# A routed expert layer on one core: the first tiles' totals and table ahead of the second part's gates, one-hot rows in halves, ties by a running count, rows three tiles ahead

## The chip, the cores and the metric

The kernel runs on one core of a Trainium2 chip. The metric is device time in microseconds; the figure before the change is the median of three runs. One further execution was taken with the hardware profiler, and all durations below come from it. Its engines are PE (TensorE, matmuls), DVE (VectorE), ACT (ScalarE), POOL (GpSimd) and SP (SyncE, which here issues DMAs).

## The reference

There are 64 x 64 = 4096 tokens of 256 values. Each token goes to the two of eight experts with the largest gates, and the result is added to the token.

```python
var = jnp.mean(x * x, axis=-1, keepdims=True)
xn = rms_w * (x * jax.lax.rsqrt(var + EPS))
gate = xn @ wg_W + wg_b + (genre_embed @ gg_W + gg_b)
gate_w = jax.nn.softmax(gate, axis=-1)
topk_w, topk_i = jax.lax.top_k(gate_w, TOP_K)
cw = jnp.sum(jax.nn.one_hot(topk_i, E, dtype=x.dtype) * topk_w[..., None], axis=-2)
h1 = jax.nn.relu(jnp.einsum('bsh,ehm->bsem', x, W1) + b1)
h2 = jax.nn.relu(jnp.einsum('bsem,emn->bsen', h1, W2) + b2)
out_e = jnp.einsum('bsen,enh->bseh', h2, W3) + b3
x + jnp.einsum('bseh,bse->bsh', out_e, cw)
```

With equal gates the expert with the smaller number is taken. H is 256, M is 512, everything is f32.

## The kernel before

**Layout.** Each of 128 partitions holds 32 tokens, so there are 32 token tiles (NI), in eight loads of four (`load j`, `xin[j]`). The first eight token tiles (two loads, NA = 8, GA = 2) are part A, the other 24 part B. Part A is routed first, so that the expert work can start on it while part B is still being routed.

**Routing.** For a load j and a half c of the 256 columns, `turn` (L183) transposes four 128x128 blocks on PE (L187) into one of the PSUM banks `TB` and copies them to a buffer `hid[:, n]` (L189 on DVE, L191 on ACT). `gates` (L193) multiplies such buffers by the gate weights; the q-th buffer writes PSUM partitions 32q to 32q+31 (L196), and the two column halves are added up there. `upright` (L204) copies the gates to `gTs` on ACT (L207) and transposes them back on PE (L210). `squares` (L176) makes a token tile's sum of squares, on ACT (L179) or on DVE (L181). `busy(n)` (L213) puts n transposes on PE whose result nobody reads (L216).

**The class Part** holds the routing of one part: `choose` (L251) scales the gates and finds the largest two in two rounds. A round takes the maximum, compares (L274), multiplies by `rank` (8 for expert 0 down to 1, L276), takes the maximum (L278) and compares again (L280), so that one expert is left of equal ones. `count` (L286) makes running counts of tokens per expert along a partition (L290), `totals` (L299) adds them over the partitions on PE (L302, L303), `pick` (L305) reads each token's place.

**The first part** (L343) does this for part A. Its table is made by one-hot rows: `ohA` (L405, 128 x 16 f16 values in each partition) says which row a token goes to, `mvA` (L406) holds its number, and 16 small matmuls (L423) sum them up in PSUM. From that DVE makes `idxA` (L425, L426), the token numbers of eight tiles of 128 tokens, one per expert. Between these steps stand the transposes, copies and gates of loads 2 to 5.

**The second part** (L428) does the transposes and gates of loads 6 and 7, the transpose of the bias vectors (`vecs`, L443, copied to `vT` by L444), and most of the sums of squares. L777 does the last four.

**The rest of part B's routing** is the generator `rest` (L456). `head_step` (L713) takes pieces of it while it works on the first seven tiles; `routing(ns)` takes pieces until their stated costs reach ns. It ends in `idxR`, the token numbers of all further tiles, and in the weights store (L328).

**The tiles.** 67 tiles of 128 tokens run in this profile: eight of part A, and 59 of the rest. For a tile, POOL gathers 128 rows of x (`gather` L585, DMA at L576) into one of three buffers `xg`, PE transposes them (L597), DVE copies them to `xTb` (L599), and PE does layer 1 (L659), layer 2 (L672) and layer 3 (L684), with ACT's relu between (L662, L675). DVE scales the result (L685), POOL adds it to the output rows by DMA (L686). From tile 8 on, DVE first copies the expert's weights (L625, L633, L644), and POOL gathers the tile's gate weights (`gather_cw` L589) that DVE reads at L647. `step(s)` (L737) issues layer 1 of tile s, the transposes of s + 1, layer 2 of s - 1, layer 3 of s - 2; its gather is that of tile s + 2. `head_step` gathers s + 3.

**Order.** In the blocks under `manual_schedule` the order of each engine's work is that of the program. That is so for the first part, the gathers of tiles 0 to 2, the second part, `busy(18)` (L788), the head steps and step 7, and again for the last steps. The steps between are ordered by a scheduler. The last tiles stand in a switch over the number of tiles.

Of the kernel before, what the change touches and what calls it, by code (L numbers as in the profile page):

```python
# [9 lines left out]
F32 = mybir.dt.float32  # L10
# [3 lines left out]
ALU = mybir.AluOpType  # L14
# [7 lines left out]
def kernel(  # L22
# [92 lines left out]
    nc.gpsimd.memset(ones, 1.0)  # L115
    rank = const.tile([P, E], F32, name="rank")
    nc.gpsimd.iota(rank, [[-1, E]], base=E, channel_multiplier=0, allow_small_or_imprecise_dtypes=True)
    tri = const.tile([P, P], F32, name="tri")
# [7 lines left out]
    nc.gpsimd.memset(segA, 1.0)  # L126
    nc.gpsimd.memset(segA[:, :, 0:1], 0.0)
    iotx = const.tile([P, P, GC], F16, name="iotx")
    nc.gpsimd.iota(iotx, [[1, P], [0, GC]], base=0, channel_multiplier=0, allow_small_or_imprecise_dtypes=True)
# [53 lines left out]
    def turn(j, c, n, eng):  # L183

        tp, xTc = TB[n], hid[:, n].rearrange("p c t -> p (c t)")
        for k in range(TPB):
            nc.tensor.transpose(tp[:, ts(k, P)], xin[j][:, k, ts(c, P)], ident)  # L187
        if eng == "V":
            V.tensor_copy(xTc, tp)  # L189
        else:  # L190
            nc.scalar.copy(xTc, tp)  # L191

    def gates(c, bufs, bank=PB[3]):  # L193

        for q, n in enumerate(bufs):
            nc.tensor.matmul(  # L196
                bank[32 * q : 32 * q + 32, :],
                lhsT=wg_sb[:, c, :],
                rhs=hid[:, n].rearrange("p c t -> p (c t)"),
                start=(c == 0),  # L200
                stop=(c == HC - 1),
            )

    def upright(nq, bank=PB[3], dst=PB[4]):  # L204

        R = 32 * nq
        nc.scalar.copy(gTs[0:R, :], bank[0:R, :])  # L207
        gtp = dst[:, 0 : TPB * R].rearrange("p (k r) -> p k r", k=TPB)
        for k in range(TPB):
            nc.tensor.transpose(gtp[:, k], gTs[0:R, ts(k, P)], ident[0:R, 0:R])  # L210
        return gtp.rearrange("p k (q e) -> p q k e", q=nq)[:, :, :, 0:E]
# [6 lines left out]
    class Part:  # L218


        def __init__(self, z, i0, i1):
            self.i0, self.i1, self.n, self.z = i0, i1, i1 - i0, z
            n = self.n
            self.t = {a: t2(f"{a}{z}", n) for a in ("var", "root", "y", "t", "rstd", "m1", "m2", "top", "den", "d2")}
# [26 lines left out]
        def choose(self, raw):  # L251

            m1, m2, top = (self.t[a] for a in ("m1", "m2", "top"))
            gate, left, rstd = self.gate, self.pr[:, 0], self.t["rstd"]
            if raw is None:
# [12 lines left out]
            for k, (g, m) in enumerate(((gate, m1), (left, m2))):  # L268
# [6 lines left out]
                yield  # L275
                V.tensor_tensor(sc, sc, self.over_i(rank), ALU.mult)  # L276
                yield
                V.tensor_reduce(top, sc, AX.X, ALU.max)  # L278
                yield
                V.tensor_tensor(sc, sc, self.over_e(top), ALU.is_equal)  # L280
                yield
# [61 lines left out]
    def first_part():  # L343
# [27 lines left out]
        V.tensor_copy(ggate, gps)  # L371
        gates(0, (0, 2))
        gates(1, (1, 3))
        pA.root()
# [12 lines left out]


        for q in range(4):
            turn(GA + q, 0, q, "A")  # L390
        gates(0, range(4))
        squares(NA, "A")
        squares(NA + 1, "A")
        for _ in pA.choose(raw):
            pass
        pA.count()
        for q in range(2):
            turn(GA + q, 1, q, "A")
        pA.totals()
        slot = pA.gate  # L400
        V.scalar_tensor_tensor(
            slot, pA.inc.rearrange("p e i -> p i e"), -1.0, pA.over_i(pA.off[:, 0, :]), ALU.add, ALU.add
        )
        pA.pick(lo16A.rearrange("p (k i) -> p k i", k=TOPK), slot)
        V.tensor_tensor(ohA, iotx, lo16A.unsqueeze(1).to_broadcast([P, P, GC]), ALU.is_equal)  # L405
        V.tensor_tensor(  # L406
# [4 lines left out]
        )  # L411
        V.tensor_copy(totA, pA.off[:, 1, :])
        for q in range(2, 4):
            turn(GA + q, 1, q, "A")
        squares(NA + 2, "A")
        gates(1, range(4))
        raw = upright(4)
        nc.scalar.copy(graw[:, NA : NA + 4 * TPB, :].rearrange("p (q k) e -> p q k e", q=4), raw)
        squares(NA + 3, "A")
        squares(NA + 4, "A")  # L420
        tabA = PB[7][:, 0:E]
        for g in range(GC):
            nc.tensor.matmul(tabA, lhsT=ohA[:, :, g], rhs=mvA[:, g, :], start=(g == 0), stop=(g == GC - 1))  # L423

        V.tensor_scalar(sa[:, 0:E], tabA, 0.0, float(NT), ALU.is_equal, ALU.mult)  # L425
        V.scalar_tensor_tensor(idxA, tabA, float(OFFA), sa[:, 0:E], ALU.add, ALU.add)  # L426

    def second_part():  # L428

        j0 = GA + 4  # L430
        for i in range(NA + 8, NI - 4):
# [9 lines left out]
        nc.scalar.copy(graw[:, j0 * TPB : NI, :].rearrange("p (q k) e -> p q k e", q=2), raw)  # L441
        vps = PB[6][:, 384 : 384 + 2 * E * MC]
        nc.tensor.transpose(vps, vecs, ident[: 2 * E * MC, : 2 * E * MC])  # L443
        V.tensor_copy(vT.rearrange("p l e c -> p (l e c)"), vps)  # L444
        for i in range(NA + 5, NA + 8):
            squares(i, "A")

# [8 lines left out]
    def rest():  # L456
# [85 lines left out]
        V.tensor_tensor(idxR, sa, sb, ALU.add)  # L542
        gather(E)
        pB.exps()
        yield 1000
# [191 lines left out]
    def step(s, last):  # L737

        if s + 2 < last:
            gather(s + 2)  # L740
        if s < last:
# [30 lines left out]
    with tc.manual_schedule():  # L772
        first_part()
        for b in range(3):
            gather(b)
        second_part()
        for i in range(NI - 4, NI):  # L777
# [9 lines left out]

        busy(18)  # L788
        routing(100)
# [66 lines left out]
```

## Time and profile before

| what | us |
|---|---|
| median of 3 runs | 543.44 (543.28 to 543.70) |
| the profiled execution's own time | 539.8 |
| its span, first to last instruction | 538.0 |
| busy PE / weight loads / DVE / ACT / POOL | 522.7 / 499.3 / 286.8 / 215.6 / 285.2 |
| mean granted PE clock | 0.994 |
| first tile's layer 1 starts | 31.92 |
| PE's last matmul starts (L684) | 525.95 |

Times in the profile count from the span's start. A line of the timeline has the start, the duration, the engine, the line of the program, the operation, out<-in by the program's names, shapes and the number of instructions merged; the bracket has the idle time of the engine before it and what ended it. An f32 matmul is two instructions, a transpose one. Matmuls overlap, so the distance from start to start says more than a duration. The timed runs lie 3.6 us above the profiled execution.

### The profile page before, as it was taken

To read this page: it belongs to the slowest core of one execution; us is meant where nothing else is said; L and a number is where in the kernel's file an instruction comes from. 1 tells how busy PE (TensorE), PEld (TensorE's weight loads), DVE (VectorE), ACT (ScalarE), POOL (GpSimd) and SP (SyncE) were. 2 spreads that over 40 slices of the span, in tenths; PEclk is the share of its full clock that TensorE was granted. 3 is DMA by queue.
4 is the path that set the end of the run, shared out by engine and by line. 5 is a ranking of instruction groups with operands and counts; after the bars stand their busy time and mean duration, and the time that the engine had idled before them with its cause. 6 is when DMAs were issued, how large, how long until landed. Compare 5 with 4: busy or idle time off the path is not lost. (4 is left out here: it accounts for less than half of the span.)

```text
span 538.0 us, 11373 instructions
## 1 busy us (share of the span) xinstructions
PE 522.7 (97%) x4136; PEld 499.3 (93%) x4136; DVE 286.8 (53%) x651; ACT 215.6 (40%) x588; POOL 285.2 (53%) x237
## 2 busy tenths in 40 slices
PE   8989999999999999999999999999999999999992
PEld 6579999999999999999999999999999999999992
DVE  4686964455455555554554545555545555454540
ACT  3754333343344434344444344344334434433430
POOL 4233668775565555556555556555556554236542
PEclk9999999999999999999999999999999999999997
DMA  8999976122222212222212221222222212222221
GB/s 272 383 393 371 367 197 177 29 41 41 41 34 31 38 33 37 39 41 31 37 28 40 41 41 26 40 32 39 31 42 34 38 28 35 30 33 39 32 22 22
DMA packets 28650, 44.45 MB, mean 83 GB/s; under 512 B 6161, under 2 KB 18530, under 8 KB 28324
## 3 DMA queue, kind: packets, MB, share of 16 engines
q0 software_dynamic: 15136, 17.32, 20.8%
q1 hardware_dynamic: 12736, 26.25, 13.8%
q8 instruction: 34, 0.56, 0.4%
q14 instruction: 36, 0.29, 0.2%
q10 hardware_dynamic: 708, 0.03, 0.1%
HBM read 35.33 MB, written 13.24 MB: 90 GB/s over the span
## 5 line engine op out<-in xcount | busy, mean ns | idle before, releaser
L672 PE MATMUL pb<-hid,big 128*128 128x128 f32 x1888 | 220.6, 275 | 0.0
L672 PEld LDWEIGHTS pb<-hid,big 128*128 128x128 f32 x1888 | 215.6, 192 | 0.3 <-ACT hid L662 0.2
L686 POOL DMA_INDIRECT out_dram<-y,idxR x59 | 106.2, 1801 | 157.4 <-DVE y L685 153.3
L675 ACT ACTIVATE hid<-pb,bb 128x128 f32<-128x128 f32 x236 | 86.8, 368 | 140.4 <-PE pb L672 96.2
L633 DVE COPY big<-w2a 128x2048 f32 x59 | 72.7, 1232 | 122.5 <-issue 75.7
L662 ACT ACTIVATE hid<-pb,bb 128x128 f32<-128x128 f32 x236 | 86.4, 368 | 121.2 <-PE pb L659 102.3
L659 PEld LDWEIGHTS pb<-xTb,big 128*128 128x128 f32 x944 | 114.7, 192 | 3.1
L659 PE MATMUL pb<-xTb,big 128*128 128x128 f32 x944 | 114.9, 275 | 0.0
L684 PE MATMUL pb<-big,hid 128*128 128x256 f32 x472 | 111.7, 379 | 0.0
L684 PEld LDWEIGHTS pb<-big,hid 128*128 128x128 f32 x472 | 85.2, 190 | 9.1
L576 POOL DMA_INDIRECT cg<-cwdR,idxR x59 | 72.5, 1229 | 21.3 <-issue 16.9
L576 POOL DMA_INDIRECT xg<-in_x_dram,idxR x59 | 60.9, 1033 | 19.7 <-issue 14.6
L599 DVE COPY xTb<-pb 128x256 f32<-128x256 f32 x67 | 28.4, 424 | 41.1 <-PE pb L597 35.7
L685 DVE SCALAR_TENSOR_TENSOR y<-pb,cw,bc 128x256 f32<-128x256 f32 x59 | 28.5, 484 | 36.0 <-PE pb L684 36.0
L625 DVE COPY big<-w1a 128x1024 f32 x59 | 41.0, 695 | 5.3 <-DVE xTb L599 0.9
L644 DVE COPY big<-w3a 128x1024 f32 x59 | 40.3, 683 | 0.0
L672 PE MATMUL pb<-hid,w2a 128*128 128x128 f32 x256 | 29.9, 275 | 0.0
L672 PEld LDWEIGHTS pb<-hid,w2a 128*128 128x128 f32 x256 | 29.2, 192 | 0.0
L597 PE MATMUL pb<-ident,xg 128*128 128x128 f32 x134 | 25.7, 273 | 0.5 <-DMA xg<-in_x_dram,idxR 0.5
L686 POOL DMA_INDIRECT out_dram<-y,idxA x8 | 14.0, 1755 | 15.5 <-DVE sli L505 7.0
L649 DVE TENSOR_SCALAR bc<-b_sb,cw 128x256 f32 x59 | 20.8, 353 | 0.4
L675 ACT ACTIVATE hid<-pb,vT 128x128 f32<-128x128 f32 x32 | 11.7, 368 | 18.7 <-PE pb L672 18.1
(184 smaller groups left out, 279.4 us busy)
## 6 DMA issues: line engine op xcount, KB each, us to landing
w2a<-in_L_cond_W_dram SPq DMA_DIRECT2D x8, 1024.0 KB
big<-in_x_dram SPq DMA_DIRECT2D x8, 512.0 KB
w1a<-in_L_cond_W_dram SPq DMA_DIRECT2D x8, 512.0 KB
w3a<-in_L_cond_W_dram SPq DMA_DIRECT2D x8, 512.0 KB
out_dram<-in_x_dram SPq DMA_DIRECT2D x4, 768.0 KB
out_dram<-in_x_dram SPq DMA_DIRECT2D x1, 1024.0 KB
b_sb<-in_L_cond_b_dram SPq DMA_DIRECT2D x1, 1024.0 KB
xg<-in_x_dram,idxR POOLq DMA_INDIRECT x59
```

The lines of the kernel that those rows point to most:

```text
L576: nc.gpsimd.indirect_dma_start(out=dst, out_offset=None, in_=src, in_offset=bass.IndirectOffsetOnAxis(ap=index(b), axis=0), bounds_check=N ...
L599: V.tensor_copy(xTb, tp)
L625: V.tensor_copy(w1, w1a[:, e].rearrange("p e c m -> p (e c) m"))
L633: V.tensor_copy(w2, w2a[:, ex[b]].rearrange("p e c m -> p (e c) m"))
L644: V.tensor_copy(w3, w3a[:, e].rearrange("p e c m -> p (e c) m"))
L659: nc.tensor.matmul(ph, lhsT=w1[:, c, ts(m, P)], rhs=xTb[:, c, :], start=(c == 0), stop=(c == HC - 1))
L662: nc.scalar.activation(h1[:, m, :], ph, AF.Relu, bias=bb[:, 0, m : m + 1])
L672: nc.tensor.matmul(ph, lhsT=w2[:, m, ts(n, P)], rhs=h1[:, m, :], start=(m == 0), stop=(m == MC - 1))
L675: nc.scalar.activation(h2[:, n, :], ph, AF.Relu, bias=bb[:, 1, n : n + 1])
L684: nc.tensor.matmul(po, lhsT=h2[:, n, :], rhs=w3[:, n, :], start=(n == 0), stop=(n == MC - 1))
L685: V.scalar_tensor_tensor(y, po, cw, bc, ALU.mult, ALU.add)
L686: add = nc.gpsimd.indirect_dma_start(out=orows, out_offset=bass.IndirectOffsetOnAxis(ap=index(b), axis=0), in_=y, in_offset=None, bounds_c ...
```

## The change

- Ties: `rank` goes. After the comparison a running count along the experts (a scan over `segT`, which is 0 at expert 0 and 1 elsewhere) numbers the equal ones, and one fused operation keeps the one with number 1.
- The gates of part A go quadrant by quadrant, both column halves of one load and then of the next.
- In the first part two ACT squares stand ahead of the transposes of loads 2 to 5. The totals stand ahead of all transposes of the second column half, `mvA` behind the totals, `ohA` is made in two halves of eight groups with eight table matmuls behind each, and the table stands ahead of the second half's gates. `totA` is copied last.
- In the second part ACT's copy to `gTs` and PE's first eight transposes stand ahead of `upright`; the transpose of `vecs` follows it, and its copy stands within the squares. Two more squares are on ACT and two fewer on DVE. `busy(2)` goes; the later `busy(18)` is `busy(16)`.
- `rest` gathers tile 9 right behind tile 8, and `step` gathers tile s + 3.

```diff
-    rank = const.tile([P, E], F32, name="rank")
-    nc.gpsimd.iota(rank, [[-1, E]], base=E, channel_multiplier=0, allow_small_or_imprecise_dtypes=True)
+    segT = const.tile([P, NB, E], F32, name="segT")
+    nc.gpsimd.memset(segT, 1.0)
+    nc.gpsimd.memset(segT[:, :, 0:1], 0.0)
...
-    def gates(c, bufs, bank=PB[3]):
-        for q, n in enumerate(bufs):
+    def gates(c, bufs, bank=PB[3], q0=0):
+        for q, n in enumerate(bufs, q0):
...
-                V.tensor_tensor(sc, sc, self.over_i(rank), ALU.mult)
+                V.tensor_tensor_scan(
+                    nth.rearrange("p i e -> p (i e)"),
+                    segT[:, 0 : self.n].rearrange("p i e -> p (i e)"),
+                    sc.rearrange("p i e -> p (i e)"),
+                    0.0,
+                    ALU.mult,
+                    ALU.add,
+                )
                 yield
-                V.tensor_reduce(top, sc, AX.X, ALU.max)
-                yield
-                V.tensor_tensor(sc, sc, self.over_e(top), ALU.is_equal)
+                V.scalar_tensor_tensor(sc, nth, 1.0, sc, ALU.is_equal, ALU.mult)
                 yield
...
-        gates(0, (0, 2))
-        gates(1, (1, 3))
+        for q in range(GA):
+            for c in range(HC):
+                gates(c, (2 * q + c,), q0=q)
...
+        some(2)
         for q in range(4):
             turn(GA + q, 0, q, "A")
         gates(0, range(4))
-        squares(NA, "A")
-        squares(NA + 1, "A")
+        some(2)
         for _ in pA.choose(raw):
             pass
         pA.count()
-        for q in range(2):
-            turn(GA + q, 1, q, "A")
         pA.totals()
...
-        V.tensor_tensor(ohA, iotx, lo16A.unsqueeze(1).to_broadcast([P, P, GC]), ALU.is_equal)
...
-        V.tensor_copy(totA, pA.off[:, 1, :])
-        for q in range(2, 4):
+        for q in range(4):
             turn(GA + q, 1, q, "A")
-        squares(NA + 2, "A")
...
+        tabA = PB[7][:, 0:E]
+        GH = GC // 2
+        for g0 in range(0, GC, GH):
+            hs = slice(g0, g0 + GH)
+            V.tensor_tensor(
+                ohA[:, :, hs], iotx[:, :, hs], lo16A[:, hs].unsqueeze(1).to_broadcast([P, P, GH]), ALU.is_equal
+            )
+            for g in range(g0, g0 + GH):
+                nc.tensor.matmul(tabA, lhsT=ohA[:, :, g], rhs=mvA[:, g, :], start=(g == 0), stop=(g == GC - 1))
+        some(3)
         gates(1, range(4))
-        raw = upright(4)
-        nc.scalar.copy(graw[:, NA : NA + 4 * TPB, :].rearrange("p (q k) e -> p q k e", q=4), raw)
-        squares(NA + 3, "A")
-        squares(NA + 4, "A")
-        tabA = PB[7][:, 0:E]
-        for g in range(GC):
-            nc.tensor.matmul(tabA, lhsT=ohA[:, :, g], rhs=mvA[:, g, :], start=(g == 0), stop=(g == GC - 1))
...
+        nc.scalar.copy(gTs, PB[3])
+        for q in range(2):
+            turn_pe(j0 + q, 0, q)
+        raw = upright(4, copied=True)
+        vps = PB[6][:, 384 : 384 + 2 * E * MC]
+        nc.tensor.transpose(vps, vecs, ident[: 2 * E * MC, : 2 * E * MC])
+        for i in range(NA + 10, NI - 4):
+            if i == NI - 8:
+                V.tensor_copy(vT.rearrange("p l e c -> p (l e c)"), vps)
             squares(i, "V")
-        for c in range(HC):
-            for q in range(2):
-                turn(j0 + q, c, 2 * c + q, "A")
+        for q in range(2):
+            turn_copy(q, "A")
+        nc.scalar.copy(graw[:, NA : NA + 4 * TPB, :].rearrange("p (q k) e -> p q k e", q=4), raw)
+        for q in range(2):
+            turn(j0 + q, 1, 2 + q, "A")
+        some(3)
         for c in range(HC):
             gates(c, (2 * c, 2 * c + 1), PB[7])
         busy(4)
         raw = upright(2, PB[7], PB[6])
-        busy(2)
         nc.scalar.copy(graw[:, j0 * TPB : NI, :].rearrange("p (q k) e -> p q k e", q=2), raw)
-        vps = PB[6][:, 384 : 384 + 2 * E * MC]
-        nc.tensor.transpose(vps, vecs, ident[: 2 * E * MC, : 2 * E * MC])
-        V.tensor_copy(vT.rearrange("p l e c -> p (l e c)"), vps)
-        for i in range(NA + 5, NA + 8):
-            squares(i, "A")
...
         gather(E)
+        gather(E + 1)
...
-        if s + 2 < last:
-            gather(s + 2)
+        if s + 3 < max(last, SURE + 1):
+            gather(s + 3)
...
-        busy(18)
+        busy(16)
```

`turn_pe` and `turn_copy` are the two halves of `turn`, and `some(n)` puts the next n squares on ACT.

More of the change, by code (lines that the diff above doesn't have):

```diff
@@ L183, in turn, with turn_pe, turn_copy @@
     def turn(j, c, n, eng):
+        turn_pe(j, c, n)
+        turn_copy(n, eng)
+    def turn_pe(j, c, n):
+        for k in range(TPB):
+            nc.tensor.transpose(TB[n][:, ts(k, P)], xin[j][:, k, ts(c, P)], ident)
+    def turn_copy(n, eng):
         tp, xTc = TB[n], hid[:, n].rearrange("p c t -> p (c t)")
-        for k in range(TPB):
-            nc.tensor.transpose(tp[:, ts(k, P)], xin[j][:, k, ts(c, P)], ident)
         if eng == "V":
@@ L202, in gates, with upright @@
             )
-    def upright(nq, bank=PB[3], dst=PB[4]):
+    def upright(nq, bank=PB[3], dst=PB[4], copied=False):
         R = 32 * nq
-        nc.scalar.copy(gTs[0:R, :], bank[0:R, :])
+        if not copied:
+            nc.scalar.copy(gTs[0:R, :], bank[0:R, :])
         gtp = dst[:, 0 : TPB * R].rearrange("p (k r) -> p k r", k=TPB)
@@ L223, in __init__ @@
             n = self.n
-            self.t = {a: t2(f"{a}{z}", n) for a in ("var", "root", "y", "t", "rstd", "m1", "m2", "top", "den", "d2")}
+            self.t = {a: t2(f"{a}{z}", n) for a in ("var", "root", "y", "t", "rstd", "m1", "m2", "den", "d2")}
             self.gate, self.w = t3(f"gate{z}", n), t3(f"w{z}", n)
@@ L251, in choose @@
         def choose(self, raw):
-            m1, m2, top = (self.t[a] for a in ("m1", "m2", "top"))
+            m1, m2 = self.t["m1"], self.t["m2"]
             gate, left, rstd = self.gate, self.pr[:, 0], self.t["rstd"]
+            nth = self.pr[:, 1]
             if raw is None:
@@ L386, in first_part, with some @@
             load_weights(e)
+        sA = iter(range(NA, NA + 10))
+        def some(n):
+            for _ in range(n):
+                squares(next(sA), "A")
+        some(2)
         for q in range(4):
@@ L396, in first_part @@
         pA.count()
-        for q in range(2):
-            turn(GA + q, 1, q, "A")
         pA.totals()
[L400 to L405, printed above, removed]
         V.tensor_tensor(
@@ L411, in first_part @@
         )
-        V.tensor_copy(totA, pA.off[:, 1, :])
-        for q in range(2, 4):
+        for q in range(4):
             turn(GA + q, 1, q, "A")
-        squares(NA + 2, "A")
-        gates(1, range(4))
-        raw = upright(4)
-        nc.scalar.copy(graw[:, NA : NA + 4 * TPB, :].rearrange("p (q k) e -> p q k e", q=4), raw)
-        squares(NA + 3, "A")
-        squares(NA + 4, "A")
-        tabA = PB[7][:, 0:E]
-        for g in range(GC):
-            nc.tensor.matmul(tabA, lhsT=ohA[:, :, g], rhs=mvA[:, g, :], start=(g == 0), stop=(g == GC - 1))
+        slot = pA.gate
@@ new lines, in first_part @@
+        V.scalar_tensor_tensor(
+            slot, pA.inc.rearrange("p e i -> p i e"), -1.0, pA.over_i(pA.off[:, 0, :]), ALU.add, ALU.add
+        )
+        pA.pick(lo16A.rearrange("p (k i) -> p k i", k=TOPK), slot)
+        tabA = PB[7][:, 0:E]
[4 more added lines that the diff above has]
+                ohA[:, :, hs], iotx[:, :, hs], lo16A[:, hs].unsqueeze(1).to_broadcast([P, P, GH]), ALU.is_equal
+            )
+            for g in range(g0, g0 + GH):
+                nc.tensor.matmul(tabA, lhsT=ohA[:, :, g], rhs=mvA[:, g, :], start=(g == 0), stop=(g == GC - 1))
@@ L425, in first_part, with second_part @@
+        some(3)
+        gates(1, range(4))
         V.tensor_scalar(sa[:, 0:E], tabA, 0.0, float(NT), ALU.is_equal, ALU.mult)
         V.scalar_tensor_tensor(idxA, tabA, float(OFFA), sa[:, 0:E], ALU.add, ALU.add)
-    def second_part():
+        V.tensor_copy(totA, pA.off[:, 1, :])
+        return some
+    def second_part(some):
         j0 = GA + 4
-        for i in range(NA + 8, NI - 4):
-            squares(i, "V")
-        for c in range(HC):
-            for q in range(2):
-                turn(j0 + q, c, 2 * c + q, "A")
+        nc.scalar.copy(gTs, PB[3])
[7 more added lines that the diff above has]
+                V.tensor_copy(vT.rearrange("p l e c -> p (l e c)"), vps)
+            squares(i, "V")
+        for q in range(2):
[4 more added lines that the diff above has]
+        some(3)
@@ L772 @@
     with tc.manual_schedule():
-        first_part()
+        some = first_part()
         for b in range(3):
             gather(b)
-        second_part()
+        second_part(some)
         for i in range(NI - 4, NI):
```

## The prediction

> **What bounds the kernel now.** I read busy time by stretch first, then TensorE's (PE's) queue over the first 32 us, then the queues of VectorE (DVE) and ScalarE (ACT) beside it, and last PE's waits in the tail. Busy time by stretch (PE, weight loads, DVE, ACT, GpSimd, granted clock, DMA):
>
> ```profile
> 20.00:30.00 10.00, 8.61 (x67) 5.65 (x65) 7.06 (x35) 6.04 (x18) 3.13 (x3) 1.00 1.05 387
> 40.00:50.00 10.00, 10.00 (x85) 9.79 (x84) 5.12 (x19) 4.37 (x13) 3.71 (x4) 1.00 1.06 370
> 50.00:60.00 10.00, 10.00 (x84) 9.79 (x83) 9.60 (x21) 4.17 (x12) 5.14 (x3) 1.00 1.07 364
> 400.00:500.00 100.00, 99.53 (x786) 96.27 (x786) 51.78 (x104) 39.24 (x108) 48.03 (x36) 1.00 0.22 34
> ```
>
> From 40 us on PE is full. So the end is set by when the first tile's matmuls (L659) start, plus PE's work from there, plus its few later waits. PE's queue ahead of that start (start, duration, line, what ended the idle time):
>
> ```profile
> 16.51 1.09 PE L187 MATMUL pb<-ident,big 128*128 128x128 f32 x8
> 17.44 0.29 PE L302 MATMUL pb<-incA,tri 128*128 128x8 f32 x2
> ...
> 18.80 1.84 PE L196 MATMUL pb<-hid,wg_sb 128*32 128x512 f32 x8
> 21.32 0.66 PE L210 MATMUL pb<-ident,gTs 128*128 128x128 f32 x4 [0.68 <-ACT gTs L207]
> 21.82 1.10 PE L423 MATMUL pb<-mvA,hotA 128*128 128x8 f16 x16
> ...
> 28.40 0.27 PE L443 MATMUL pb<-ident,vecs 64*128 64x64 f32 x1 [0.30 <-ACT graw L441]
> 29.00 2.19 PE L216 MATMUL pb<-ident 128*128 128x128 f32 x18 [0.33 <-DVE vT L444]
> 31.02 0.38 PE L597 MATMUL pb<-ident,xg 128*128 128x128 f32 x2
> 31.92 2.05 PE L659 MATMUL pb<-xTb,w1a 128*128 128x128 f32 x16 [0.52 <-DVE xTb L599]
> ```
>
> The totals (L302) and the table (L423) come late because other PE work stands ahead of them, and the last stretch before L597 is 18 filler transposes and waits. The same stretch on DVE:
>
> ```profile
> 16.50 0.29 DVE L290 TENSOR_TENSOR_SCAN incA<-segA,prA 128x64 f32<-128x64 f32 x1
> 18.04 0.27 DVE L401 SCALAR_TENSOR_TENSOR gateA<-incA,pb 128x64 f32<-128x64 f32 x1 [1.25 <-PE pb L303]
> ...
> 18.99 1.22 DVE L405 TENSOR_TENSOR hotA<-iotx,lo16A 128x2048 f16<-128x2048 f16 x1
> 20.14 0.28 DVE L406 TENSOR_TENSOR mvA<-ohA,toka 128x128 f16<-128x128 f32 x1
> ...
> 22.95 0.17 DVE L425 TENSOR_SCALAR sa<-pb 128x8 f32<-128x8 f32 x1 [2.46 <-PE pb L423]
> ```
>
> DVE waits 1.25 us for totals and 2.46 us for the table; idxA is written at 23.33. Then 16 sums of squares, one each 0.465 us (23.24, 23.70, 24.16), hold DVE until 30.7. So PE and DVE reach the first tile together: PE's transpose ends 31.40, DVE's copy starts 31.44. Both must get earlier, and the change moves both. The tail has one wait:
>
> ```profile
> 493.38 0.44 PE L597 MATMUL pb<-ident,xg 128*128 128x128 f32 x2 [0.47 <-DMA xg<-in_x_dram,idxR]
> ```
>
> [...]
> - [...] between 15.10 and 15.20 five gate matmuls of 0.59 to 0.62 us are in flight. Four starting at once no run here shows.
> - [...] 2048 elements take 1.22 us, 1104 take 0.72 (L523), so 0.53 ns an element and 0.13 fixed. Half of L405 (1024 elements) is then 0.68.
> - [...] from 64 to 192 elements the scan goes from 0.29 to 0.56, a multiply from 0.23 to 0.36.
> - [...] The trace has clock 1.00 throughout the head, with idle gaps up to 0.68; the gaps I expect are under 0.6, so I charge no clock.
>
> **The change, step by step** (times of the profiled execution; "start to start" where instructions overlap).
>
> 1. *Gates of the first tiles by quadrant.* The second quadrant's first matmul starts at 9.77, right after buffer 2 is copied (9.72), and four in a row end at 11.67. In the new order it waits for the same copy: gain 0. Bounds: 0.2 later, if it queues behind the first quadrant's loads, to 0.2 earlier. The constants on GpSimd (one iota of 0.13 out, two memsets of 0.25 and 0.10 in) end before 6.6, where DVE still waits for wg_in: 0.
>
> 2. *Ties by a count.* Per round, multiply, max and compare (13.88 to 14.65, 0.77) become a scan (0.33 start to start) and one fused operation (0.26): 0.18 saved, 0.36 in two rounds. incA ends 16.43 instead of 16.79. The same for 24 tiles in pB saves about 0.4 where DVE later waits for PE anyway (3.42 us ahead of L477): 0. There the counting step slips into the step of tile 1; pB's totals keep their place on PE.
>
> 3. *Two ACT squares ahead of the copies.* ACT is idle 1.14 us ahead of 13.43; two squares take 2 x 0.54 = 1.08 from 12.19. They fit: the copies stay at 13.43 to 15.48. If not, every copy moves by what is over, some 0.1.
>
> 4. *Totals ahead of the transposes.* PE is free at 16.51, the counts are there at 16.5: totals from 16.53, 0.51 long. L401 goes from 18.04 to about 17.13. mvA (0.28) moves into DVE's wait, so it costs nothing; uncovered it would be 0.28. The 16 transposes of the second column half follow at 16.93 and take 1.87, to 18.80. Behind them wait only ACT's copies, 17.6 to 19.7.
>
> 5. *Table in halves, ahead of the second gates.* L401 to L405 took 0.95: halves from 18.08 to 18.76 and 19.43. PE is free at 18.80, takes eight matmuls at 0.062 each, waits, and does the others from 19.49 to about 20.1. idxA ends at 20.58 instead of 23.33: 2.75 earlier. Bounds of a half: 0.68, or 1.22 if rows of 8 out of 16 lose the double rate; then the table ends 1.1 later. I take 0.68[...].
>
> 6. *Second gates with all copies done.* Before, they took 1.84 because each waited for its copy. Now four column groups can start at once: 0.454 + 0.592 = 1.05, from 20.1 to 21.2. Bounds: 1.05, or 1.95 if only two run together. I take 1.05.
>
> 7. *Second part.* From 21.12 PE does eight transposes (0.93), upright (0.49), vecs (0.15) and eight transposes (0.95), to 23.65. ACT's copy of the gates (L207, 0.58) goes ahead of its turn copies, so upright no longer waits (0.68 before). The last gates take 23.72 to 25.62 (1.9; 24.65 to 26.60 before). A new wait: three squares on ACT (24.33 to 25.95) stand ahead of the last L207, which so runs 25.87 to 26.45 and holds PE some 0.25 more. Upright to 26.96, ACT's graw copy to 27.22, and as fillers and graw share a PSUM bank (the waits of L443 and L216 above) the 16 fillers begin 27.27: 1.81. L597 at 29.08; L659 0.90 later, **29.98 against 31.92: 1.94 earlier**. The 2 fillers fewer there, and the 2 behind upright, are in this.
>
> 8. *DVE by then.* After idxA: totA 0.2, 14 squares 6.5, vT 0.2: free at 27.5, L239 and L314 until 27.9. PE's transpose ends 29.46, so DVE has 1.5 us to spare. GpSimd's three gathers follow idxA and run about 20.9 to 24.6, long ahead of 29.08.
>
> 9. *Rows three tiles ahead.* In the steady state a gather is issued soon after its buffer is free (109.67 after the transposes of 105.38), so nothing moves. In the hand-ordered tail the gather that L597 waits for is issued only at 489.65; issued a step (7.3) earlier it no longer holds PE. L659 to L659 is 8.00 there (490.96 to 498.96), 7.31 elsewhere: 0.69, of which 0.05 may stay. I take **0.64**, bounds 0 to 0.7. The extra gather behind idxR (1.0 + 0.3 us of GpSimd) stands ahead of the adds of tiles 3 and 4, of the weights store and of SP's copies that wait for those adds; all have later users. Cost 0, or one DVE stall up to 0.9.
>
> Sum: 1.94 + 0.64 = 2.6 off the profiled execution's 539.8 us (span 538.0): 537.2. The runs' median is 543.44, 3.6 above that; I take the same difference off: **540.8**.
>
> **Rivals.**
> - *The head gains half.* Slow halves (1.1), gates in pairs (0.9), or one of them with a late ACT. For: neither form is in the trace. Against: [...] three groups seen together. Gain 2.6 - 1.0 = 1.6: 541.8.
> - *The head's gain is given back.* Between 50 and 70 DVE is nearly full, and xTb of tile 5 is copied at 64.01 to 64.43 for matmuls at 64.81: 0.39 of margin. If that chain is held by anything but PE's totals, PE waits there and only the tail's 0.64 stays: 542.8. Against: DVE starts it after waiting 3.42 us for exactly those totals.
> - *Slower: GpSimd's queue.* A gather three tiles ahead needs the buffer of a tile just transposed. If it stands ahead of adds and weight gathers and waits, DVE's copy of cw waits (11.2 us in four waits already), the w2 copy (L633) behind it too, and PE's L672: at 103.97 that copy ends 105.20 for matmuls at 105.60. Over some 52 steps 0.05 us each eats the whole gain; 0.1 each gives 5.2 - 2.6, thus 546.0. Against: in steady state gathers already follow their buffer.
>
> **How the numbers follow.** Forecast 0.68, half the head 0.15, given back 0.07, slower 0.10. This measurement can tell 0.2% (1.09 us) from no change, so faster means below 542.35: the forecast and nearly all of the first rival, 0.82; same 0.09, the given-back case and the rest; slower 0.09. The range goes from 539.9 (ACT's squares cost nothing, gates 0.2 earlier, 0.3 of reading error) to 542.6 (slow halves and paired gates, tail gained).
>
> **What would show it.** Right: L302 near 16.5, idxA written near 20.6, second gates about 1.05 us, L659 near 30.0, no wait for xg in the tail, pace 7.31. Wrong: halves above 0.8, gates near 1.9, DVE late for the first xTb, a step above 7.31, or new PE waits between 50 and 115 us.

## The result, and the profile after

| | before | after |
|---|---|---|
| median of 15 runs each | 541.64 us (538.94 to 543.85) | 538.37 us (537.96 to 539.05) |
| ratio, 95% interval | | 0.9939 (0.9923 to 0.9955) |
| profiled execution, own time | 539.8 | 538.7 |
| its span | 538.0 | 537.0 |

The change makes the kernel 0.61% faster, about 3.3 us; the forecast had 2.6. The predicted time, 540.8, is 2.4 us above what was measured, which lies below the range too (539.9 to 542.6). Most of that is the base: the three runs shown at first (543.28 to 543.70) lay high in a spread of 5 us, in which 52 later runs of the same kernel have their median at 541.72. That spread turns out to be the main thing that the change removes.

PE's queue of the changed kernel in the head, from its timeline (start, duration, engine, line, operation; the bracket is the idle time ahead and what ended it):

```profile
17.17 0.36 PE L316 MATMUL pb<-incA,tri 128*128 128x8 f32 x2
...
19.54 1.26 PE L440 MATMUL pb<-mvA,hotA 128*128 128x8 f16 x16
20.73 1.07 PE L203 MATMUL pb<-hid,wg_sb 128*32 128x512 f32 x8
21.73 1.09 PE L191 MATMUL pb<-ident,big 128*128 128x128 f32 x8
22.66 0.60 PE L218 MATMUL pb<-ident,gTs 128*128 128x128 f32 x4
...
24.42 1.05 PE L203 MATMUL pb<-hid,wg_sb 128*32 128x512 f32 x4
25.71 1.80 PE L203 MATMUL pb<-hid,wg_sb 128*32 128x512 f32 x4 [0.24 <-issue]
...
29.19 1.97 PE L224 MATMUL pb<-ident 128*128 128x128 f32 x16 [0.30 <-ACT graw L472]
30.99 0.38 PE L624 MATMUL pb<-ident,xg 128*128 128x128 f32 x2
31.89 0.82 PE L686 MATMUL pb<-xTb,w1a 128*128 128x128 f32 x5 [0.52 <-DVE xTb L626]
```

Totals (L316), table (L440) and second gates (L203 at 20.73) stand in the new order, the gates in 1.07 instead of 1.84 us. And yet the first layer (L686) starts at 31.89, where it started at 31.92. In this execution PE's very first transposes began at 7.52 us, before at 6.81. The kernel before itself varies so (7.17, 7.45 and 6.83 in three more profiles with its head), so it belongs to the run, and the head is better measured from its first gates. Before and after:

```profile
9.00 2.67 PE L196 MATMUL pb<-hid,wg_sb 128*32 128x512 f32 x8
```

```profile
9.59 2.68 PE L203 MATMUL pb<-hid,wg_sb 128*32 128x512 f32 x8
```

From there it is 22.30 us to the first layer instead of 22.92, a gain of 0.62. This mark is steady: in the seven profiles with the old head the stretch takes 22.89 to 22.92. On DVE:

```profile
16.73 0.29 DVE L304 TENSOR_TENSOR_SCAN incA<-segA,prA 128x64 f32<-128x64 f32 x1
...
17.84 0.27 DVE L428 SCALAR_TENSOR_TENSOR gateA<-incA,pb 128x64 f32<-128x64 f32 x1 [0.64 <-PE pb L317]
...
18.79 1.29 DVE L436 TENSOR_TENSOR hotA<-iotx,lo16A 128x1024 f16<-128x1024 f16 x2
...
21.04 0.17 DVE L445 SCALAR_TENSOR_TENSOR idxA<-pb,sa 128x8 int32<-128x8 f32 x1
```

`idxA` is written at 21.21 (23.33 before), and the two halves of `ohA` take 1.29 us together. In the tail the line that had an idle bracket of 0.47 has none:

```profile
492.48 0.38 PE L624 MATMUL pb<-ident,xg 128*128 128x128 f32 x2
```

Comparing the starts of layer 1 from tile to tile in the two profiles leaves three differences: the start above, the step to tile 9 (7.52 before, 7.31 after) and the tail's step (8.00 before, 7.31 after). All other steps agree within 0.05 us.

### The profile page after: what moved, and what is told of

Same layout as the page of the kernel before. It is cut to its first block, busy times and chain, and to the rows that moved or that the text cites. A ratio compares the mean times of both kernels' runs of the same rounds, so it can differ in the third digit from the quotient of the medians.

```text
span 537.0 us, 11366 instructions
## 1 busy us (share of the span) xinstructions
PE 522.7 (97%) x4132; PEld 499.4 (93%) x4132; DVE 285.4 (53%) x644; ACT 216.8 (40%) x592; POOL 286.3 (53%) x238
## 4 chain that ended last, share of the span: by engine, by line
PE 96%; DVE 1%; DMA 1%; issue 1%; POOL 0%; ACT 0%; POOLq 0%; DVEq 0%
PE pb L699 44%; PE pb L686 22%; PE pb L711 21%; PE pb L624 3%; PE pb L224 1%; PE pb L191 1%; PE pb L203 1%; PE pb L480 1%; DMA out_dram<-y,idxR 1%; DVE sqV L182 0%; POOL out_dram L713 0%; PE pb L218 0%; PE pb L440 0%; ACT gTs L215 0%; DVE big L671 0%
## 5 line engine op out<-in xcount | busy, mean ns | idle before, releaser
L686 PEld LDWEIGHTS pb<-xTb,big 128*128 128x128 f32 x944 | 114.7, 192 | 3.0
L686 PE MATMUL pb<-xTb,big 128*128 128x128 f32 x944 | 114.9, 275 | 0.0
L603 POOL DMA_INDIRECT xg<-in_x_dram,idxR x59 | 62.0, 1051 | 19.6 <-issue 15.6
```

Source lines behind the costliest of these rows:

```text
L603: nc.gpsimd.indirect_dma_start(out=dst, out_offset=None, in_=src, in_offset=bass.IndirectOffsetOnAxis(ap=index(b), axis=0), bounds_check=N ...
L686: nc.tensor.matmul(ph, lhsT=w1[:, c, ts(m, P)], rhs=xTb[:, c, :], start=(c == 0), stop=(c == HC - 1))
```

## The experiments

There were two theories at first. A: the tail and the rows' timing hold most of the gain and the spread. B: the forecast as it stands.

**The rows alone, the head alone.** `e1_rows` is the kernel before with this, `e2_head` the changed kernel without it:

```diff
         gather(E)
+        gather(E + 1)
...
-        if s + 2 < last:
-            gather(s + 2)
+        if s + 3 < max(last, SURE + 1):
+            gather(s + 3)
```

> The kernel before with one part of the change alone: rows gathered three tiles ahead (tile 9's gather behind tile 8's, and each step gathers s + 3). Theory A (most of the gain is in the tail, where the late gather also makes the runs of before differ by some 5 us): about 3 us faster than before, and the runs within 1.5 us of each other. Theory B (the forecast: 1.9 in the head, 0.6 in the tail, the spread comes from elsewhere): 0.6 faster, the spread of before stays. In both the trace has no wait for xg in the tail and layer 1 at a pace of 7.31 there; the first tile's layer 1 stays near 31.9.

Measured: 539.08 us (538.53 to 539.58), ratio 0.9966 (0.9953 to 0.9978).

> The changed kernel without the rows three tiles ahead (gather of s + 2 and no early gather of tile 9, as before): the reordered head alone. Theory A: no faster than before by more than 0.5 us, and the spread of before, 5 us, comes back. Theory B: 2 us faster, and narrow or wide like before for a cause in the head. In both the wait for xg in the tail is back.

Measured: 540.93 us (540.19 to 542.92), ratio 1.000 (0.9981 to 1.0019). So the rows gain 1.8 us (1.2 to 2.5), less than the 3 of theory A but more than the tail's 0.69, and take the spread away; the head alone shows no gain. The kernel before was profiled once more to see where its slower runs lose time:

> The kernel before, unchanged, for a second profiled execution and more times: its runs so far lie between 538.9 and 543.9 us and the one profile at 539.8. Theory A: in a longer execution the tail's wait for xg is longer than 0.47 us. Theory B: in a longer execution the first tile's layer 1 starts later than 31.9 us and the tail's wait is the same.

Measured: 542.36 us (539.51 to 544.54), ratio 1.0013 (0.9986 to 1.0040). Its profile is the key to the case. PE around tile 9's transposes (L597), in that profile:

```profile
89.02 1.95 PE L659 MATMUL pb<-xTb,big 128*128 128x128 f32 x16
93.46 0.44 PE L597 MATMUL pb<-ident,xg 128*128 128x128 f32 x2 [2.49 <-DMA xg<-in_x_dram,idxR]
```

and in the profile of before that the prediction was made from:

```profile
90.72 0.44 PE L597 MATMUL pb<-ident,xg 128*128 128x128 f32 x2
```

PE waits 2.49 us for tile 9's rows in one execution and hardly in the other; the steps to tile 9 are 10.01 and 7.52, where 7.31 is the usual pace. The rows are asked for by the gather at 88.38 and 87.64, and an SP copy from the input to the output (a fill, L735) is issued at nearly the same time. From the timeline of all engines, first the new profile of before, then the one at first:

```profile
88.38 1.01 POOL L576 DMA_INDIRECT xg<-in_x_dram,idxR  x1 [0.31 <-issue]
88.45 0.51 SPq L735 DMA_DIRECT2D out_dram<-in_x_dram  x1
```

```profile
87.64 1.06 POOL L576 DMA_INDIRECT xg<-in_x_dram,idxR  x1 [0.31 <-issue]
88.37 0.51 SPq L735 DMA_DIRECT2D out_dram<-in_x_dram  x1
```

What the DMA engines then did, in the DMA view (queue, kind: packets, MB, share of 16 engines). The new profile, from 90.5 to 92 us:

```profile
DMA packets 93, 0.57 MB, mean 381 GB/s; under 512 B 0, under 2 KB 0, under 8 KB 93
...
q1 hardware_dynamic: 93, 0.57, 98.3%
```

The one at first, from 89 to 90.5 us:

```profile
q1 hardware_dynamic: 18, 0.11, 46.6%
q0 software_dynamic: 48, 0.13, 31.5%
```

q0 carries the gathers (its 0.13 MB here are the 128 rows of 1 KB), q1 the fills. With 0.73 us of lead the rows' packets start at 89.41 and are through at 90.3, while the fill begins at 89.8. With 0.07 us of lead the fill is first (89.8 to 92.6) and the rows' packets start only at 92.3. The lead has to be more than nothing because a gather's first packet comes 1.8 us after its issue (87.64 to 89.41) and a fill's 1.3 to 1.4 (88.45 to 89.77); from these the gather must be issued some 0.4 us ahead to be first, which is an estimate. The traces show this order, not what sets it. A fill is 768 KB in packets of some 6 KB (93 of them are 0.57 MB), and the view from 90.5 to 92 us has no packet of q0.

In the one profile of `e2_head` the fill is issued at 87.61, ahead of the gather at 87.80, and PE waits again:

```profile
92.89 0.69 PE L623 MATMUL pb<-ident,xg 128*128 128x128 f32 x2 [2.23 <-DMA xg<-in_x_dram,idxR]
93.37 5.11 PE L698 MATMUL pb<-hid,w2a 128*128 128x128 f32 x32
```

That the head's 0.62 us shows nowhere fits such a wait in most runs: none of the 14 is under 540.19 us, where 15 of the 40 runs of the kernel before beside them are. But only this profile shows it. (The tail's wait, which both theories expected back, is not in it: the step is 7.43.)

The same profile shows that the wait can cost more than its length. Behind it layer 2 (L698) takes 5.11 us instead of 3.74, and the step to tile 9 is 11.33 instead of the 10.01 above, because the granted clock fell. Busy time by stretch (the number ahead of the last two is the granted clock):

```profile
94.00:96.00 2.00, 2.00 (x12) 2.00 (x11) 1.92 (x5) 0.37 (x1) 1.70 (x2) 0.50 0.11 12
```

Such a fall can be read from a run's mean clock: in the profiles of before and after the clock falls to 0.50 some 3 us behind PE's last matmul (from 531 and 529 us on), and the profiles with one more fall ahead of the end have 0.989 to 0.992, all others 0.993 to 0.996. Of the 138 runs of the kernel before that were made with the experiments, 42 have 0.992 or less, with a median of 543.45 us; the other 96 have a median of 540.6. Of 66 runs of the kernels that ask for tile 9's rows early or leave out the last fill (the changed kernel and `e1_rows`, `e4_tile9`, `e9_nofill4` below) none is so low. By this the upper part of the spread is the wait with a fall of the clock behind it.

**Which gather?** Theory A now names the wait for tile 9. `e4_tile9` asks for tile 9's rows early and leaves all else; `e5_tail` does the rest and leaves tile 9 where it was:

```diff
         gather(E)
+        gather(E + 1)
...
-        if s + 2 < last:
+        if s + 2 < last and s + 2 != E + 1:
             gather(s + 2)
```

> The kernel before with one thing of the change: the rows of tile 9 are asked for beside those of tile 8, not one step later; all other gathers stay two steps ahead. Theory A (the wait for tile 9's rows, 0.2 to 2.7 us long from one run to the next, is most of what the change gains): the step to tile 9 takes 7.3 us in the profile, the last step of the tail still 8.0; the median falls by about 1.9 of the 2.5 us that rows three ahead gained, to some 0.35% under the kernel before (ratio about 0.9965 to 0.998), and the runs stand within 1.2 us of each other. Theory B (the forecast: an early gather of tile 9 costs nothing and gains nothing, the tail's 0.64 us is the gain): ratio 1.000, and the runs spread over 4 to 5 us as those of the kernel before do.

Measured: 539.58 us (538.78 to 540.35), ratio 0.9959 (0.9943 to 0.9974). The step to tile 9 is 7.31, the tail keeps its wait:

```profile
493.18 0.44 PE L598 MATMUL pb<-ident,xg 128*128 128x128 f32 x2 [0.47 <-DMA xg<-in_x_dram,idxR]
```

> The kernel before with the other half: rows three tiles ahead from tile 10 on, but tile 9's rows still asked for in the step of tile 7. Theory A: the last step of the tail falls from 8.0 to 7.3 us, the step to tile 9 keeps its wait of 0.2 to 2.7 us, the runs still spread over 4 to 5 us; median 0.7 us under the kernel before (ratio about 0.9987). Theory B: the whole gain of rows three ahead is here, the 0.64 us of the forecast or more (ratio 0.9966 if it is to make up what that experiment measured).

Measured: 539.41 us (538.65 to 543.37), ratio 0.9975 (0.9956 to 0.9995). The tail's step is 7.31, and tile 9 waits in the profile:

```profile
93.05 0.44 PE L597 MATMUL pb<-ident,xg 128*128 128x128 f32 x2 [2.29 <-DMA xg<-in_x_dram,idxR]
```

The runs fall into two groups, 11 of 20 at 538.65 to 539.6 and nine at 540.2 to 543.4. So A holds: one gather of 128 rows asked for 11.5 us earlier (76.15 instead of 87.64) takes the spread away (1.6 us instead of 5) and is worth 0.41%, or 2.2 us (1.4 to 3.1). The median of `e5_tail` is lower than A said (ratio 0.9987), though the interval includes that. Its step no longer lets tile 10's gather go ahead of tile 9's, so the rows may have been first more often; this was not tested. In its profile a lead of 0.28 us (87.55 against 87.83) was not enough.

**Is it the fill?** `e6_fills` issues the four fills one head step earlier:

```diff
-        if s >= E - 1 - NF:
-            i = NA + (s - (E - 1 - NF)) * (NB // NF)
+        if E - 2 - NF <= s < E - 2:
+            i = NA + (s - (E - 2 - NF)) * (NB // NF)
```

> The kernel before with its four copies of 768 KB from the input to the output issued one step earlier, so that the last of them goes at about 82 us and none at 88. Theory A with a collision as its mechanism (tile 9's rows, asked for at 88 us, stand behind the packets of the fourth copy): the step to tile 9 is 7.3 to 7.5 us in the profile, the runs draw together, and the median is 1 to 2 us under the kernel before (ratio about 0.9965 to 0.998). Its rival, the gather is late by itself, since it stands last in its step's GpSimd queue: the step to tile 9 stays at 7.5 to 10, ratio 1.000, same spread.

Measured: 542.37 us (541.12 to 544.77), ratio 1.0007 (0.9991 to 1.0024), and a step to tile 9 of 11.82, with a wait of 2.67 us and the clock at 0.50 behind it. The expectation failed. The last fill, now from 85.1 to 88.1, holds up tile 10's rows and then GpSimd's adds and weight gathers; DVE waits 8.7 us for gate weights (three waits), and tile 9's gather is issued at 90.58, 2.9 us later than before. The fill takes the engines for some 3 us here too (89.8 to 92.6 above), so this run doesn't tell the two readings apart. `e9_nofill4` does: the kernel before without the fourth fill, so that a part of the output is left unfilled, and the first three in their places.

```diff
-        if s >= E - 1 - NF:
+        if E - 1 - NF <= s < E - 2:
```

> The kernel before without its fourth copy of 768 KB from the input to the output (the one issued at 88 us), so that part of the output isn't filled; everything else as before. Theory A with the collision (tile 9's rows stand behind that copy's packets whenever their gather is issued less than about half a us ahead of it): no wait of over 0.2 us at tile 9, the step to tile 9 7.3 to 7.5 us, the runs within 1.2 us of each other, and a median about 1.9 us under the kernel before, near 539.6 (ratio 0.995 to 0.998). Rival (the gather is late by itself): step to tile 9 up to 10 us, spread of 4 to 5 us, ratio 1.000.

Measured: 539.53 us (539.22 to 541.24), ratio 0.9960 (0.9945 to 0.9976), step to tile 9 7.50, 14 of 15 runs within 1.2 us. With the gather issued at 87.54, as late as ever, the long wait is gone: the collision with the fill is shown. What is left, 7.50 instead of 7.31, is the gather's own lateness.

**The fillers.** Fillers are the transposes of `busy`, whose result nobody reads; they are meant to keep PE's clock up. `e3_nofill` is the changed kernel with one filler ahead of tile 0's transposes:

```diff
-        busy(16)
+        busy(1)
```

> The changed kernel with one filler transpose ahead of the first tile's transposes instead of 16. The trace of after has DVE and GpSimd done by 28.6 us while PE's fillers run to 30.99. If PE alone holds the first tile there, layer 1 starts 15 x 0.11 = 1.6 us earlier and the kernel is 1.6 us faster than the changed one. If something else is as late (the first rows' gather, DVE, weights), less; if the clock falls for lack of fillers, slower.

Measured: 536.90 us (536.62 to 538.14), ratio 0.9923 (0.9897 to 0.9950). The first layer starts at 29.59, and 1.7 us nearer to the first gates (20.62 instead of 22.30), but the next step takes 4.47 instead of 2.83. From busy time by stretch:

```profile
29.00:30.00 1.00, 0.48 (x4) 0.41 (x4) 0.82 (x3) 0.99 (x2) 0.65 (x1) 0.95 1.02 401
30.00:31.00 1.00, 1.00 (x6) 1.00 (x6) 0.88 (x5) 0.63 (x3) 0.35 (x1) 0.50 1.02 393
31.00:32.00 1.00, 1.00 (x7) 1.00 (x6) 0.30 (x1) 0.37 (x1) 0.75 (x3) 0.50 1.07 410
```

In this execution the clock fell, and that took back nearly all that the 15 fillers fewer had gained. That was not so in most runs: this was the slowest of the six runs (538.14 us, mean clock 0.989), and the other five have 0.994 to 0.996 and 536.62 to 537.25 us. `e7_warm` puts fillers into waits that are there anyway:

```diff
-        busy(4)
+        busy(8)
         raw = upright(2, PB[7], PB[6])
...
-        busy(16)
         routing(100)
         stage_1(0)
         transpose_x(0)
+        busy(4)
```

> The changed kernel with the 16 filler transposes ahead of tile 0's own transposes taken out, as in the run with one filler, but with four of them put behind tile 0's transposes (there PE waits 0.5 us for VectorE's copy) and eight in place of four ahead of the last gate transposes. In the run with one filler the first layer began 2.3 us earlier than in the changed kernel, and then the clock granted fell to half for 3 us and the first step took 4.5 in place of 2.8 us. Theory C (fillers in waits keep the clock at no cost): first layer at about 29.7 us, first step 2.8, span 535 to 535.5, median 1.3 to 1.6 us under the run with one filler (about 535.5). Rival: 12 fillers in the waits are too few, the clock falls all the same and the median is that of one filler, 536.9.

Measured: 536.14 us (535.86 to 537.39), ratio 0.9893 (0.9864 to 0.9923). First layer at 29.11, next step 2.83, clock 1.00:

```profile
29.00:30.00 1.00, 1.00 (x10) 0.90 (x9) 0.86 (x6) 0.99 (x2) 0.86 (x1) 1.00 0.96 383
30.00:31.00 1.00, 1.00 (x12) 1.00 (x11) 0.79 (x4) 1.00 (x5) 0.26 (x1) 1.00 1.05 404
```

So theory C's first layer and first step are there. The median came out 0.6 us above what it said, since it had reckoned with the fall of the clock in every run of `e3_nofill`. That twelve fillers are what keeps the clock is likely but not shown: its six runs and the twelve of two later versions with fillers in the waits have mean clocks of 0.993 to 0.996, against one fall in six runs with one filler.

**PE's late releases.** In the changed kernel's ACT queue something else stands out:

```profile
22.43 1.08 ACT L198 COPY hid<-pb 128x512 f32<-128x512 f32 x2
24.32 0.27 ACT L464 COPY graw<-pb 128x128 f32<-128x128 f32 x1 [0.81 <-PE pb L191]
25.07 0.59 ACT L198 COPY hid<-pb 128x512 f32<-128x512 f32 x1 [0.49 <-PE pb L191]
25.83 0.59 ACT L198 COPY hid<-pb 128x512 f32<-128x512 f32 x1 [0.17 <-PE pb L203]
```

`graw` waits for `upright`, whose last transpose ends at 23.26 as the profile models it, but is released at 24.29; the last two copies are 1.0 and 1.3 us behind their transposes (24.05, 24.49). In the old head copies follow within 0.05. Theory D: it comes with `upright` between the transposes. `e8_order` is `e7_warm` with

```diff
-            turn_pe(j0 + q, 0, q)
+            turn(j0 + q, 0, q, "A")
+        for q in range(2):
+            turn(j0 + q, 1, 2 + q, "A")
+        gates(0, (0, 1), PB[7])
         raw = upright(4, copied=True)
...
+        some(1)
         nc.scalar.copy(graw[:, NA : NA + 4 * TPB, :].rearrange("p (q k) e -> p q k e", q=4), raw)
...
+        some(2)
+        gates(1, (2, 3), PB[7])
...
```

> The version with fillers in the waits (e7_warm), with PE's order in the second part changed: the sixteen transposes of loads 6 and 7 stand together again, as in the kernel before, and upright, the bias transpose follow behind the first two last gates; ACT makes the four copies in a row. In the changed kernel, the run with one filler and e7_warm ACT waits 0.7 to 1.3 us longer for PE here than PE's modelled ends say, from upright on. Theory D (those late releases come with upright standing between the transposes): with the transposes together each copy follows its transposes within 0.05 us, as in the kernel before, the last gates end at about 25.6 instead of 26.8, and the first layer starts at 28.1 to 28.4 instead of 29.1, held then by VectorE's squares: median about 0.8 us under e7_warm (535.3). Theory E (PE is late here whatever its order): the copies are released 0.7 to 1.3 us late again, the first layer starts at 28.8 to 29.2 and the median is that of e7_warm (536.1).

Measured: 536.41 us (536.07 to 536.80), ratio 0.9904 (0.9880 to 0.9928). In its profile the releases are on time, four copies in a row:

```profile
22.31 2.06 ACT L198 COPY hid<-pb 128x512 f32<-128x512 f32 x4
25.19 0.27 ACT L466 COPY graw<-pb 128x128 f32<-128x128 f32 x1 [0.41 <-PE pb L218]
```

Nothing is gained, as DVE now waits 1.55 us for the bias transpose, which comes later, and copies the first `xTb` at 29.49. `e10_best` moves that DVE copy behind its ten squares; `e11_order16` is the same with the change's own 4 and 16 fillers:

```diff
         for i in range(NA + 10, NI - 4):
-            if i == NI - 8:
-                V.tensor_copy(vT.rearrange("p l e c -> p (l e c)"), vps)
             squares(i, "V")
+        V.tensor_copy(vT.rearrange("p l e c -> p (l e c)"), vps)
```

> The version with PE's transposes together (e8_order) with one thing more: VectorE's copy of the bias vectors stands behind its ten squares, not behind six of them. In e8_order PE gave every release within 0.05 us and tile 0's transposes ended at 28.1, but VectorE waited 1.5 us for the bias transpose that now comes later, did its squares until 29.2 and copied the first xTb only at 29.49. Theory D (releases on time, VectorE the last one): without that wait VectorE is free at about 28.0, the first xTb is copied right behind PE at about 28.15, the first layer starts at about 28.65 if PE's first transposes are as late as in e8_order (7.5 to 8.1 us), 28.0 if as early as in e7_warm: median about 535.0, ratio near 0.988. Rival (VectorE or ScalarE is held by something else): first layer at 29.3 or later, median 536 or more.

Measured: 535.64 us (535.15 to 536.07), ratio 0.9880 (0.9854 to 0.9907), first layer at 28.44: the fastest version, 1.2% (0.9 to 1.5) under the kernel before.

> The changed kernel with its fillers as they are (4 and 16), but the second part's order of e10_best: sixteen transposes together, upright and bias transpose behind the first two last gates, the bias copy behind ten squares. It sets apart what late releases took from the forecast's 1.94 us. Theory D: tile 0's transposes start at about 29.7 instead of 31.0, the first layer at 30.5 to 30.7 instead of 31.89, median about 1.2 us under the changed kernel (537.1). Theory E (the order is indifferent as long as 16 fillers stand ahead): first layer at 31.5 or later, median 538.2 to 538.5.

Measured: 537.62 us (537.41 to 537.98), ratio 0.9916 (0.9890 to 0.9943), first layer at 30.98, 21.57 us from the first gates (22.30 in the changed kernel). The order is worth 0.7 us. But theory D falls: in `e10_best` the third and fourth copies are 1.1 and 1.4 us behind their transposes again, and up to there its PE program is that of `e8_order`; in `e11_order16` three are late. It was not the order. Theory F, the weights' traffic, was tried in `e12_quiet` (the changed kernel), `e13_quiet_order` (`e11_order16`) and `e14_quiet_best` (`e10_best`): all SP transfers from the second expert's weights on wait for DVE's last square, by way of a reload of one token tile that waits for it.

```diff
         load_weights(0)
-        load_weights(1)
...
             squares(i, "V")
+        nc.sync.dma_start(xin[NG - 1][:, TPB - 1, :], xr[:, NI - 1, :])
+        load_weights(1)
...
```

> The changed kernel with its DMA engines left quiet from about 19 to 28 us: the weights of the second expert and all that follow on SP's queue (the first fill, the biases, the other experts) wait for VectorE's last sum of squares. What is asked is whether PE's releases in the second part are late because of that traffic. In six of seven profiles with the new head ACT waited 0.7 to 1.4 us longer than PE's modelled ends say, once the bus was full of weights. Theory F (the traffic, [...] holds PE): releases within 0.1 us of the modelled ends, copies at about 22.4, 22.9, 24.1 and 24.6, the first layer at about 30.8 in place of 31.89 (0.6 less if PE starts as early as in the kernel before). Theory E (late whatever the traffic): copies at about 25.1 and 25.8 again, first layer at 31.9.

Measured: copies at 22.25, 22.73, 24.96 and 25.71, with the DMA engines at 0.24 of their time from 22 to 24 us instead of 1.05:

```profile
24.17 0.27 ACT L458 COPY graw<-pb 128x128 f32<-128x128 f32 x1 [0.84 <-PE pb L191]
24.96 0.58 ACT L198 COPY hid<-pb 128x512 f32<-128x512 f32 x1 [0.52 <-PE pb L191]
```

> The same quiet stretch, in the version with the transposes together and the changed kernel's fillers. With full traffic its copies stood 0.7, 1.0 and 1.35 us behind the modelled ends. Theory F: all four copies within 0.1 us of the modelled end or of the copy ahead (0.48 us apart), first layer at about 30.4 in place of 30.98. Theory E: two or three copies 0.7 to 1.4 us late, first layer at 31.0.

Measured: copies at 21.82, 22.30, 23.70 and 24.46, the last two 1.05 and 1.4 us late; first layer at 30.54, 21.54 us from the first gates, as in `e11_order16`.

> The same quiet stretch, in the fastest version so far. With full traffic its third and fourth copies stood 1.06 and 1.4 us behind the modelled ends. Theory F: all four copies 0.48 us apart, first layer at about 28.0 in place of 28.44 (PE starting early as there). Theory E: two or more copies late, first layer at 28.4. In all three kernels the later weights come some 8 us late, so that PE may wait for them in the steps of tiles 2 to 7, and the total says nothing; only the first 32 us are read.

Measured: copies at 22.43, 22.91, 24.32 and 25.10, two of them late; first layer at 29.08, 19.49 us from the first gates, as in `e10_best` (19.48). (One run each, 540.71, 541.77 and 543.42 us: PE waits for weights later on.) Theory F falls as well. Nine of ten profiles with the new head have the late releases (`e8_order` is the tenth), none of seven with the old one. What makes them stays open.

## Why the forecast was wrong, step by step

The times after are given less the 0.59 us by which PE's first gates started later.

1. *Gates by quadrant*, 0: right, they end at 11.69 (11.67 before).
2. *Ties by a count*, incA at 16.43: 16.43.
3. *Two squares in ACT's gap*: right, the copies stand at 13.44 (13.43).
4. *Totals*: L428 said 17.13, measured 17.25.
5. *Halves* at 0.68, idxA at 20.58: 0.69 each, 1.29 for the two, 20.62. Rows of 8 out of 16 kept the rate of the whole L405 (2048 elements in 1.22), which was assumed, not shown, until then; the bounds for slow halves were not needed.
6. *Second gates* 1.05: 1.07. By the modelled ends all eight matmuls (two for each block of 32 PSUM partitions, 0.59 to 0.62 us each) are in flight from 21.25 to 21.40, so the four groups do run at once here.
7. *Second part*, L659 at 29.98: 31.30. **Mis-sized:** 1.94 became 0.62. The first of the last gates start at 23.83 (said 23.72), the others only at 25.12, since ACT's copies were released up to 1.3 us late. From there all is late by the same amount: gTs 27.22 instead of 25.87, fillers 28.60 instead of 27.27; the fillers take 1.80 as said. I had added up PE's modelled durations; what its consumers see came later.
8. *DVE free* at 27.9: 27.95.
9. *Tail* 0.64: 0.69, right. ***"The extra gather ... Cost 0, or one DVE stall up to 0.9"* is a step that failed.** It was counted only as a burden. It is the largest part of the gain, the wait for tile 9, 2.2 us in the median (`e4_tile9`). The profile at hand showed its trace, a step of 7.52, and I read "7.31 elsewhere".

In sum 0.62 + 0.69 + 2.2 = 3.5 us, against 3.3 measured (2.4 to 4.2).

**The predicted time failed at the step behind the sum, *"The runs' median is 543.44, 3.6 above that; I take the same difference off"*.** For the profiled execution the forecast was 537.2 us, 1.5 too low (538.7 measured; 1.3 of it is the head). The 3.6 us did not stay: the changed kernel's runs have their median 0.3 us below its profiled execution, so 3.9 us went there, and 3.9 less 1.5 are the 2.4 by which the time came out lower. The difference was no property of the profile but in the main the wait for tile 9, which this one execution had escaped; I carried it along without a reason. In the second profile of before, 2.9 us longer, 2.49 of them are that wait. The three runs at first lie where in the later series 35 of 36 runs (those above 543 us) have a mean clock of 0.992 or less, so most likely they had the fall of the clock as well; over 15 runs the difference is 1.8 us, not 3.6. That the gain came out near the forecast is luck: 1.3 us too much in the head stood against 2.2 left out.

The rivals: the head did gain less than half, but not for slow halves or paired gates. The gain was not given back between 50 and 115 us, and no step became longer behind GpSimd's queue.

## What to carry to other kernels

When timed runs lie well above the profiled one, or spread widely, do not carry the difference along as a constant. Look in the profile for a transfer that just made it: a gather issued within a us of a large copy that uses the same DMA engines (here leads of 0.07 and 0.28 us lost, one of 0.73 won). Of two profiles of the same kernel one had a wait of 2.49 us and the other hardly any, so one profile doesn't show its price; asking for the rows a step earlier removed both wait and spread here. The mean clocks of the timed runs tell more than one profile does. Fillers that are to hold the clock belong in waits that exist anyway, not ahead of the instruction that all wait for: with twelve in waits the kernel took 536.14 us (`e7_warm`), with 4 and 16, the 16 ahead of tile 0's transposes, 538.37.

## What the runs showed of the hardware

- A 768 KB copy within DRAM held the 16 DMA engines for 2.8 us (89.8 to 92.6), and the rows of a 128 KB gather issued 0.07 us ahead of it had no packet before 92.3 (`b1_before`; from 90.5 to 92 the copy's queue has 98.3% of the engines' time). With 0.73 us of lead the gather's first packets came ahead of the copy's (89.41 and 89.8, the profile of before).
- The clock fell to 0.50 behind a wait of PE of 2.23 us (`e2_head`, 0.50 from 94 to 96 us) and one of 2.67 us (`e6_fills`), but not behind waits of 2.29 (`e5_tail`, mean clock 0.996) and 2.49 us (`b1_before`, 0.995). With one filler (`e3_nofill`) it fell, in one of six runs, after PE had been at 0.70 and 0.48 of its time for 2 us (28 to 30), and stayed down for some 3.4 us, an estimate from its 0.95, 0.50 and 0.95 in the stretches 29 to 30, 30 to 33 and 33 to 36 us. By the modelled ends no idle piece from 28 to 30 us is above 0.52 us (29.08 to 29.59), so this fall came without a long gap. With twelve fillers in waits the clock stayed at 1.00 (`e7_warm`, 28 to 36 us).
- With the new head PE's completions reached ACT 0.7 to 1.4 us after the modelled ends over some 2 us of dense f32 transposes, in nine of ten profiles, with the DMA engines at 1.05 of their time (the changed kernel, 22 to 24 us) or at 0.24 (`e12_quiet`). With the old head, whose sixteen transposes stand as densely, they came within 0.05 us in all seven, so it is not the transposes alone. The releases, not the modelled ends, are what to count with.
